# Layer 1 of a two-layer graph network: seven instead of four row tiles a group with head 0's product as an exponential of logs, 19 instead of 22 tiles summed by transfer

## The chip, the cores and the metric

The kernel runs on one core of a Trainium2 chip. The metric is the device time of one execution in microseconds (us). The core's engines each have their own instruction queue: PE (TensorE) multiplies matrices, DVE (VectorE) and ACT (ScalarE) work on tiles element by element, POOL (GpSimd) does too and issues transfers, SP (SyncE) issues transfers. PEld is PE's loading of weights. Everything is in float32.

## The reference, cut to what matters

The change is in layer 1, a graph attention with 8 heads over 4096 nodes. `data` is the layer's normalised input, `connectivity` is `adj` itself, added to the logits.

```python
N, IN_DIM, H, D = (4096, 512, 8, 64)
data1 = (data @ W.T + b).reshape(N, H, D)
src = jnp.einsum('nhd,xhd->nh', data1, src_proj)
trg = jnp.einsum('nhd,xhd->nh', data1, trg_proj)
e = src.T[:, :, None] + trg.T[:, None, :]
e = jnp.where(e >= 0, e, 0.01 * e)
e = e + connectivity[None, :, :]
scores = jax.nn.softmax(e, axis=-1)
out = jnp.einsum('hnm,hmd->hnd', scores, data1.transpose(1, 0, 2))
```

So the numerator of the softmax for head h, target n and source m is exp(leaky(src[n,h] + trg[m,h])) * exp(adj[n,m]). The kernel needs, for each head, its product with `data1` and its sum over m.

## The kernel before, in words

Layer 0 and the linear part of layer 1 take the first 1,660 us and aren't touched. Then comes the attention of layer 1, which the change is in. The work is cut into 8 groups: 4 blocks `b` of WL = 1024 targets, times 2 halves `g` of 4 heads (HG). A group walks over NT = 32 row tiles `m` of 128 sources each. One pair (group `i`, tile `m`) is a step, and the steps of all groups form one long list.

The order of the work is written out by hand: each engine executes its instructions in the order in which the program names them. `stages` says which function runs in a step and how many steps ahead of that step's tile: `load` 4 steps ahead, `exps` 1, `weigh` 1, `factors` 2, `logs` at the step itself, `scale` 2, `gather` 0. In a step s of a group this gives:

- `load` (SP): the tile of `adj_t` four steps ahead into e (4 buffers); in some steps also the next group's z rows (steps 3 and 4, counted by the tile that is loaded) and the next group's u row, broadcast over the partitions (when the tile loaded is 28).
- `exps` (ACT, L1061): ex = exp(adj) of tile s+1, into PSUM, one buffer.
- `weigh` (DVE) of tile s+1: the products pr3, pr0, pr1, pr2 of the four heads, in this order. Heads 1 to 3 are max(z, g_m) times ex (L1107), where head 3 uses e3, an exp with a bias. Head 0 is (rl - ngd_m) * ex (L1104). pr0 has three buffers, pr1 to pr3 have two.
- Also in `weigh`, on POOL: acc3 += pr3 (L1116), and head 0's running sum by transfer: for the tiles in `BY_DMA`, a transfer with an adding write puts pr0 onto one of two accumulators acc00 and acc01 in turn (L1120 for the first two tiles, L1122 for the rest).
- `factors` (ACT) of tile s+2: e3 (L1071), then rl, a relu of z with scale and bias (L1089).
- For the tiles that are keys of `BY_LOG`, head 0 goes another way. `logs` writes lg, a relu of u (the logarithm's part that depends on both, L1078), on ACT in the step that `BY_LOG` names, and a transfer on POOL's queue adds the tile of `adj_t` to it in place (L1079). Two steps ahead of the tile, `relus` takes exp(lg + t_m) straight into pr0 (ACT, L1086) instead of writing rl, and DVE has three products for this tile, not four. lg has one buffer.
- `scale`: in groups 0 and 1 alone, the values of two heads are multiplied by d_m (ACT, L1057, or POOL for the first tiles).
- `gather` (PE) of tile s: 16 matmuls of 32 output columns each for the values (L1139, each is two instructions of the trace), and sums with 2 columns (L1144, `dn`): those of heads 1 and 2 for all tiles, that of head 0 for the tiles that are not in `BY_DMA` (weights `zo`). `side`, the parity of how many such tiles came before, says which half of the output partitions goes first. At the last tile PE also sums the accumulators.

At a group's end ACT copies the four banks of values (os, L1172) and, a step later, dn (od, L1178). The output of a group is finished during the next group: in the steps that `PARTS` names PE transposes (`pt`, L1198; pd, L1182, from od), DVE takes a reciprocal (rd, L1186), ACT scales four pieces (o, L1225) and transfers add x and write out. PE's transposes come behind the gathers of steps 1, 2, 6, 11 and 18, and the four o are written in steps 3, 4, 7, 8, 12, 13, 19 and 20. Group 0 has no such predecessor and makes tables instead, mostly in its first ten steps.

Of the kernel before, what the change touches and what calls it, by code (L numbers as in the profile page):

```python
# [8 lines left out]
FP = mybir.dt.float32  # L9
AF = mybir.ActivationFunctionType  # L10
ALU = mybir.AluOpType
# [4 lines left out]
P = 128  # L16
# [6 lines left out]
def row_bcast(ap, n, offset=0):  # L23

    return bass.AP(tensor=ap.tensor, offset=ap.offset + offset, ap=[[0, P], [1, n]])
# [3 lines left out]
def kernel(  # L29
# [15 lines left out]
    nc = tc.nc  # L45
    N, F = x.shape
    H, D = 8, 64
    HG, WL = 4, 1024
    WT = WL // P
    NT = N // P  # L50
# [14 lines left out]
    u_d = dram.tile([2, NT, P], FP, name="u_d")  # L65
# [39 lines left out]
    with tc.tile_pool(name="w0", bufs=1) as wp, tc.tile_pool(name="a0", bufs=2) as ap_, tc.tile_pool(  # L105
        name="a0s", bufs=8
# [355 lines left out]
    with tc.tile_pool(name="mx", bufs=1) as mxp, tc.tile_pool(name="b_a", bufs=6) as adjp, tc.tile_pool(  # L462
        name="b_e", bufs=1
    ) as esp, tc.tile_pool(name="b_m", bufs=4) as mkp, tc.tile_pool(name="b_s", bufs=2) as sp, tc.tile_pool(
        name="b_p", bufs=6, space=PSUM
# [11 lines left out]
        def load(i, j, t):  # L477
            w, lo, sk = parts(i, j, t)
            rows = slice(t * P, (t + 1) * P)
            ar = adjp.tile([P, BL], FP, name="ar")  # L480
            nc.sync.dma_start(ar[:, :w], adj[rows, lo:lo + w])
            ac = adjp.tile([P, BL], FP, name="ac")
            nc.sync.dma_start(ac[:, :w], adj_t[rows, lo:lo + w])
            loaded[i, j, t] = ar, ac
# [36 lines left out]
        for n in range(-6, len(items)):  # L521
            for f, ahead in ((load, 6), (mask, 1), (scores, 0)):
                if 0 <= n + ahead < len(items):
                    f(*items[n + ahead])
            if n >= 0:
                i, j, t = items[n]
                if j == NB - 1 and t % TB == TB - 1 and i < NB - 1:
                    ends[n + 2] = ends[min(n + 5, len(items) - 2)] = ends[min(n + 7, len(items) - 1)] = \
                        maxima(i, accs[i], p_x, sp)
                    if i < KEEP:  # L530
                        extra.append(support_sums((7, 6, 4)[i // 2], i % 2))
                next(ends.get(n, iter(())), None)
                if extra and next(extra[0], 0) == 0:
                    extra.pop(0)
                if (i, j) == (1, 3) and t % TB == TB - 1:
                    nc.sync.dma_start(mb_0, row_bcast(mx_d[0], BL))
# [7 lines left out]
    with tc.tile_pool(name="c_a", bufs=7) as adjp, tc.tile_pool(name="c_e", bufs=9) as etp, tc.tile_pool(  # L544
        name="c_d", bufs=5
    ) as wkp, tc.tile_pool(name="c_t", bufs=2) as atp, tc.tile_pool(name="c_u", bufs=2) as smp, tc.tile_pool(
        name="c_m", bufs=2
    ) as mxp, tc.tile_pool(name="c_o", bufs=4) as iop, tc.tile_pool(name="c_v", bufs=1) as cvp, tc.tile_pool(
        name="c_s", bufs=2
# [61 lines left out]
        def weigh(b, m):  # L611
            d, i = ex.pop((b, m)), m - b * TB
            if m % 2 == 0:
                at[b, m // 2] = atp.tile([P, 2, BL], FP, name="at")
            w = at[b, m // 2]
            nc.vector.tensor_tensor(w[:, m % 2, :], d, aj.pop((b, m)), ALU.mult)  # L616
            if m == 0:
                racc = blk[b][1] = mxp.tile([P, BL], FP, name="racc")
                nc.gpsimd.memset(racc, 0.0)
            racc, c0 = blk[b][1], max(i + 1, 0) * P  # L620
            if c0 < BL:
                nc.gpsimd.tensor_tensor(racc[:, c0:], racc[:, c0:], d[:, c0:], ALU.add)  # L622
# [247 lines left out]
        def gather(b, m):  # L870
# [5 lines left out]
            elif b:  # L876
                products(b - 1, NT // 2 - 1, PR[NF:])

        stages = ((load, 11), (load_a, 7), (gather, 0), (turn, 5), (exps, 4), (more_sums, 1), (weigh, 2), (sums, 2),
                  (residuals, 0))  # L880
        z = bank(PR[-1])
        pc = column_maxima(acc_z, z)
        dens = iter(())
        for s in range(-11, end):
            b, m = divmod(s, NT)
# [88 lines left out]


    PARTS = (0, 1, 2, 3, 4, 6, 7, 8, 11, 12, 13, 18, 19, 20, 22)
    BY_LOG = {10: 5, 16: 10, 22: 16, 27: 22}
    BY_DMA = [m for m in range(NT) if m not in (4, 7, 13, 14, 19, 23, 24, 25, 29, 31)]

    with tc.tile_pool(name="p", bufs=2) as prp, tc.tile_pool(name="rl", bufs=2) as rlp, tc.tile_pool(  # L980
        name="io1", bufs=2
    ) as iop, tc.tile_pool(name="s1", bufs=1) as sp, tc.tile_pool(name="za", bufs=1) as zp0, tc.tile_pool(name="e3", bufs=2) as e3p, tc.tile_pool(
        name="zb", bufs=1
    ) as zp1, tc.tile_pool(name="e", bufs=4) as ep, tc.tile_pool(name="ac", bufs=2) as acp, tc.tile_pool(
        name="os", bufs=1
    ) as osp, tc.tile_pool(name="u", bufs=1) as usp, tc.tile_pool(
        name="p_x", bufs=1, space=PSUM
    ) as p_x, tc.tile_pool(name="p_v", bufs=1, space=PSUM) as p_v, tc.tile_pool(
        name="p_t1", bufs=1, space=PSUM
    ) as p_t, tc.manual_schedule():  # L990
        groups = [(b, g) for b in range(N // WL) for g in range(H // HG)]
        steps = [(i, m) for i in range(len(groups)) for m in range(NT)]
        us = {}
        zs_, ra, ex, e3, rl, pr, acc, pv, late = {}, {}, {}, {}, {}, {}, {}, {}, {}
# [35 lines left out]
        def zload(i, k):  # L1030
            b, g = groups[i]
            zs_[i, k] = (zp1 if i % 2 else zp0).tile([P, WL], FP, name=f"z{k}")
            nc.sync.dma_start(zs_[i, k], row_bcast(z_d, WL, (g * HG + k) * N + b * WL))

        def load(i, m):
            b, g = groups[i]
            e = ep.tile([P, WL], FP, name="e")
            nc.sync.dma_start(e, adj_t[m * P:(m + 1) * P, b * WL:(b + 1) * WL])
            ra[i, m] = e
            if i + 1 < len(groups) and m == 28:  # L1040
                us[i + 1] = usp.tile([P, WL], FP, name="u")
                b, g = groups[i + 1]
                nc.sync.dma_start(us[i + 1], row_bcast(u_d, WL, g * N + b * WL))
            m0, n = (3, 2) if i else (22, 1)
            if i + 1 < len(groups) and m0 <= m < m0 + HG // n:
                for k in ORDER[n * (m - m0):n * (m - m0) + n]:
                    zload(i + 1, k)
# [26 lines left out]
        def logs(i, s):  # L1074
            for m in [m for m in BY_LOG if BY_LOG[m] == s]:
                b, g = groups[i]
                r = rlp.tile([P, WL], FP, name="lg", bufs=1)
                nc.scalar.activation(r, us[i], AF.Relu, bias=nlg_m[:, g, m:m + 1], scale=-(1.0 - SLOPE))  # L1078
                nc.gpsimd.dma_start(r, adj_t[m * P:(m + 1) * P, b * WL:(b + 1) * WL], accum_op=ALU.add)  # L1079
                rl[i, m] = r  # L1080

        def relus(i, m):
            h = groups[i][1] * HG
            if m in BY_LOG:
                pr[i, m, 0] = prp.tile([P, WL], FP, name="pr0", bufs=3)
# [6 lines left out]
        def weigh(i, m, order=ORDER):  # L1092
            h = groups[i][1] * HG
            x_ = ex.pop((i, m))
            for k in order:
                if (i, m, k) in pr:
                    continue
                w = prp.tile([P, WL], FP, name=f"pr{k}", bufs=3 if k == 0 else 2)
                if k == 0 and (i, m) == (0, 0):
                    r = rlp.tile([P, WL], FP, name="rl")  # L1100
                    nc.vector.tensor_scalar(r, zs_[0, 0], g_m[:, 0, 0:1], d_m[:, 0, 0:1], ALU.max, ALU.mult)
                    nc.vector.tensor_tensor(w, r, x_, ALU.mult)
                elif k == 0:
                    nc.vector.scalar_tensor_tensor(w, rl.pop((i, m)), ngd_m[:, h // HG, m:m + 1], x_,  # L1104
                                                   op0=ALU.subtract, op1=ALU.mult)
                else:
                    nc.vector.scalar_tensor_tensor(w, zs_[i, k], g_m[:, h + k, m:m + 1],  # L1107
                                                   e3.pop((i, m)) if k == 3 else x_,
                                                   op0=ALU.max, op1=ALU.mult)
                pr[i, m, k] = w  # L1110
            w = pr[i, m, 3]
            if m == 1:
                acc[i, 3] = acp.tile([P, WL], FP, name="acc3", bufs=1)
                nc.gpsimd.tensor_tensor(acc[i, 3], pr[i, 0, 3], w, ALU.add)
            elif m > 1:
                nc.gpsimd.tensor_tensor(acc[i, 3], acc[i, 3], w, ALU.add)  # L1116
            if m == 1:
                for n in range(2):
                    acc[i, 0, n] = acp.tile([P, WL], FP, name=f"acc0{n}", bufs=1)
                    nc.gpsimd.dma_start(acc[i, 0, n], pr[i, n, 0])  # L1120
            elif m > 1 and m in BY_DMA:
                nc.gpsimd.dma_start(acc[i, 0, BY_DMA.index(m) % 2], pr[i, m, 0], accum_op=ALU.add)  # L1122

        def gather(i, m):
            b, g = groups[i]
# [4 lines left out]
            v, dn = pv[i]  # L1130
            by_pe = [u for u in range(NT) if u not in BY_DMA]
            side = sum(u < m for u in by_pe) % 2
# [143 lines left out]


        load(0, 0)
        for k in ORDER:
            zs_[0, k] = zp0.tile([P, WL], FP, name=f"z{k}")  # L1280
# [28 lines left out]
        for g in range(H // HG):  # L1309
            nc.gpsimd.tensor_copy(d0_m[:, 2 * g:2 * g + 2, :, 0], d_m[:, HG * g + 1:HG * g + 3, :])  # L1310
        nc.gpsimd.tensor_copy(d0_0[:, :, 0], d0_m[:, :, 0, 0])
        weigh(0, 0, (3, 1, 2, 0))
        scale(0, 0)
        factors(0, 1)
        scale(0, 1)

        stages = ((load, 4), (exps, 1), (weigh, 1), (factors, 2), (logs, 0), (scale, 2), (gather, 0))
        for s in range(len(steps)):
            for f, ahead in stages:
# [48 lines left out]
```

## Time and profile before

| what | value |
|---|---|
| time before, median of 3 runs | 2880.13 us (2878.46 to 2880.64) |
| the profiled execution's own time | 2878.71 us |
| its span, first to last instruction | 2876.9 us |
| PE, DVE, ACT, POOL busy over the span | 2770.8, 2610.5, 1391.4, 1533.9 us |
| layer 1's attention, from first `pv` matmul | from 1672 us to the end |
| L1107 and L1104, DVE, one product of 128 x 1024 | 1.27 us, starts 1.19 us apart |
| L1078 and L1086, ACT, 32 each | 1.135 us |
| L1079, transfer onto lg, 32 | 512 KB each |
| L1120 and L1122, transfer of pr0 onto acc, 16 and 160 | 512 KB each, 5.8 us to landing |

The profile shows one execution. Busy times of an engine are the union of its instructions; an instruction's time includes the part in which the next one already runs, so starts can be closer than durations. A wait is idle time of an engine just before an instruction, with the instruction or transfer that ended it. A transfer's time to landing runs from its issue to the arrival of its last part.

### The profile page before, as it was taken

What the parts mean: (1) busy time and instruction counts of PE and PEld (TensorE: products, weight loads), DVE (VectorE), ACT (ScalarE), POOL (GpSimd) and SP (SyncE); (2) the same over time, 40 slices, a digit from 0 to 9 for tenths busy, and PEclk for the clock granted to TensorE, in tenths of its full rate; (3) what the DMA queues carried; (4) which work ended last, traced back from release to release, by engine and by line L of the source; (5) the groups of instructions that cost most, each with busy time, mean ns of one, the idle gap of its engine ahead of it and who ended that gap; (6) DMA issues with size and microseconds to landing.
All of it is one profiled execution on the core that took longest, in us unless ns stands there. A gap on an engine that the chain in (4) does not pass through costs nothing.

```text
span 2876.9 us, 47763 instructions
## 1 busy us (share of the span) xinstructions
PE 2770.8 (96%) x16859; PEld 1486.0 (52%) x16859; DVE 2610.5 (91%) x3694; ACT 1391.4 (48%) x2116; POOL 1533.9 (53%) x1320
## 2 busy tenths in 40 slices
PE   7999999997999999999998979999999999999998
PEld 4885444444888878878875424322222222222222
DVE  7877798898898898899995799999999999999998
ACT  2212233332223322322321078887878777878786
POOL 5323444443244345345454766676757675757675
PEclk9999999998999999999999989999999999999999
DMA  5538798887999876766754179898989898989896
GB/s 179 175 89 289 249 343 300 292 299 205 199 192 215 224 171 193 210 179 191 207 151 132 51 203 246 237 241 234 235 236 243 234 242 237 241 240 239 212 230 170
DMA packets 528321, 622.60 MB, mean 216 GB/s; under 512 B 294136, under 2 KB 346392, under 8 KB 528080
## 3 DMA queue, kind: packets, MB, share of 16 engines
q1 hardware_dynamic: 461488, 413.00, 48.4%
q0 software_dynamic: 64576, 202.61, 29.8%
q10 hardware_dynamic: 2016, 3.93, 0.4%
q8 instruction: 132, 2.16, 0.3%
q14 instruction: 109, 0.89, 0.1%
HBM read 421.01 MB, written 106.10 MB: 183 GB/s over the span
## 4 chain that ended last, share of the span: by engine, by line
PE 70%; DVE 16%; DMA 6%; issue 5%; ACT 2%; SPq 1%; DVEq 0%; POOL 0%; ACTq 0%; POOLq 0%
PE pv L1139 26%; PE pe L501 14%; PE po L669 11%; PE dn L1144 8%; PE bank L269 6%; PE po L809 4%; DVE pr L1107 4%; DVE at L616 3%; DMA et<-er_d 2%; DVE d L608 2%; DVE u L637 1%; DMA a<-in_adj_t_dram 1%; SPq L581 1%; ACT e L1071 1%; DMA et<-ec_d 1%
## 5 line engine op out<-in xcount | busy, mean ns | idle before, releaser
L1139 PE MATMUL pv<-pr,sup 128*32 128x512 f32 x8192 | 1020.7, 594 | 14.0 <-DMA e<-in_adj_t_dram 10.9
L1116 POOL TENSOR_TENSOR acc<-acc,pr 128x1024 f32<-128x1024 f32 x240 | 572.8, 2387 | 311.5 <-DVE pr L1107 309.8
L1107 DVE SCALAR_TENSOR_TENSOR pr<-z,g_m,ex 128x1024 f32<-128x1024 f32 x512 | 630.1, 1270 | 0.0
L1139 PEld LDWEIGHTS pv<-pr,sup 128*32 128x32 f32 x8192 | 294.0, 110 | 608.7 <-issue 564.7
L609 ACT ACTIVATE d<-d 128x512 f32<-128x512 f32 x256 | 161.1, 630 | 542.1 <-DVE d L608 321.4
L501 PE MATMUL pe<-he_t,he_t 128*128 128x512 f32 x896 | 386.4, 592 | 0.0
L1061 ACT ACTIVATE ex<-e 128x1024 f32<-128x1024 f32 x256 | 263.3, 1028 | 241.7 <-DVE pr L1107 239.2
L1144 PE MATMUL dn<-pr,d_m 128*2 128x512 f32 x1984 | 344.7, 592 | 0.0
L1107 DVE SCALAR_TENSOR_TENSOR pr<-z,g_m,e 128x1024 f32<-128x1024 f32 x256 | 327.3, 1279 | 0.0
L1071 ACT ACTIVATE e<-e,ld_m 128x1024 f32<-128x1024 f32 x256 | 290.7, 1135 | 0.0
L1104 DVE SCALAR_TENSOR_TENSOR pr<-rl,ngd_m,ex 128x1024 f32<-128x1024 f32 x223 | 283.2, 1270 | 1.9 <-ACT ex L1061 1.6
L501 PEld LDWEIGHTS pe<-he_t,he_t 128*128 128x128 f32 x896 | 169.2, 190 | 208.4 <-issue 192.6
L1089 ACT ACTIVATE rl<-z,ngd_m,d_m 128x1024 f32<-128x1024 f32 x223 | 273.8, 1228 | 0.0
L616 DVE TENSOR_TENSOR at<-d,a 128x512 f32<-128x512 f32 x256 | 215.4, 842 | 54.7 <-PE po L669 44.7
L669 PE MATMUL po<-he_t,at 128*128 128x256 f32 x1024 | 263.9, 380 | 0.0
L669 PE MATMUL po<-sup,u 128*128 128x256 f32 x1024 | 262.8, 379 | 0.0
L669 PE MATMUL po<-sup,at 128*128 128x256 f32 x1024 | 244.3, 381 | 13.4 <-DVE at L616 13.4
L622 POOL TENSOR_TENSOR racc<-racc,d 128x512 f32<-128x512 f32 (+2 forms) x136 | 181.0, 1331 | 96.5 <-ACT d L609 91.3
L669 PEld LDWEIGHTS po<-sup,at 128*128 128x128 f32 x1024 | 195.3, 191 | 41.3 <-DVE at L616 14.7
L669 PEld LDWEIGHTS po<-sup,u 128*128 128x128 f32 x1024 | 194.7, 190 | 26.6
L669 PEld LDWEIGHTS po<-he_t,at 128*128 128x128 f32 x1024 | 193.5, 190 | 28.1 <-DVE sc L689 2.3
L506 POOL DMA_DIRECT2D er_d<-mk x136 | 74.4, 547 | 234.8 <-DVE rm L503 227.0
(261 smaller groups left out, 3748.7 us busy)
## 6 DMA issues: line engine op xcount, KB each, us to landing
e<-in_adj_t_dram SPq DMA_DIRECT2D x256, 512.0 KB, 5.9
acc<-pr POOLq DMA_DIRECT2D x176, 512.0 KB, 5.8
a<-in_adj_t_dram SPq DMA_DIRECT2D x256, 256.0 KB, 3.6
ar<-in_adj_dram SPq DMA_DIRECT2D x120, 256.0 KB, 4.8
ac<-in_adj_t_dram SPq DMA_DIRECT2D x120, 256.0 KB, 5.1
ec_d<-mc POOLq DMA_DIRECT2D x120, 256.0 KB, 4.8
et<-ec_d SPq DMA_DIRECT2D x120, 256.0 KB, 3.5
er_d<-mk POOLq DMA_DIRECT2D x112, 256.0 KB, 4.2
```

The lines of the kernel that those rows point to most:

```text
L501: nc.tensor.matmul(pe[:, :w], he_t[i][:, k, (t % TB) * P:(t % TB + 1) * P], he_t[j][:, k, BL - w:], start=(k == 0), stop=(k == KC - 1))
L616: nc.vector.tensor_tensor(w[:, m % 2, :], d, aj.pop((b, m)), ALU.mult)
L622: nc.gpsimd.tensor_tensor(racc[:, c0:], racc[:, c0:], d[:, c0:], ALU.add)
L669: nc.tensor.matmul(acc[:, j, :], A[:, j * P:(j + 1) * P], B, start=(first_ and j == 0), stop=last, skip_group_check=True)
L1061: nc.scalar.activation(x_, ra.pop((i, m)), AF.Exp)
L1071: nc.scalar.activation(x_, ra[i, m], AF.Exp, bias=ld_m[:, h // HG, m:m + 1])
L1089: nc.scalar.activation(r, zs_[i, 0], AF.Relu, bias=ngd_m[:, h // HG, m:m + 1], scale=d_m[:, h, m:m + 1])
L1104: nc.vector.scalar_tensor_tensor(w, rl.pop((i, m)), ngd_m[:, h // HG, m:m + 1], x_, op0=ALU.subtract, op1=ALU.mult)
L1107: nc.vector.scalar_tensor_tensor(w, zs_[i, k], g_m[:, h + k, m:m + 1], e3.pop((i, m)) if k == 3 else x_, op0=ALU.max, op1=ALU.mult)
L1116: nc.gpsimd.tensor_tensor(acc[i, 3], acc[i, 3], w, ALU.add)
L1139: nc.tensor.matmul(v[c][q][r * D + c0:r * D + c0 + Q, :], va[:, m, g * HG + k, c0:c0 + Q], pr[i, m, k][:, q * BL:(q + 1) * BL], start=(m = ...
L1144: nc.tensor.matmul(dn[r * Q:r * Q + w.shape[1], :], w, src[:, q * BL:(q + 1) * BL], **fl)
```

## The change

The table `BY_LOG` gets seven tiles (6, 10, 14, 19, 22, 26, 30), with the steps in which their lg is written (1, 5, 9, 14, 17, 21, 25), in place of four. `BY_DMA` leaves out thirteen tiles instead of ten, so that 19 of 32 are summed by transfer. A group's u row is loaded along with its own first tile, which is four steps later than before, since the last lg of the group before is now written in step 25. The index of the accumulator counts so that the last tile summed by transfer goes onto acc01, as before.

```diff
     PARTS = (0, 1, 2, 3, 4, 6, 7, 8, 11, 12, 13, 18, 19, 20, 22)
-    BY_LOG = {10: 5, 16: 10, 22: 16, 27: 22}
-    BY_DMA = [m for m in range(NT) if m not in (4, 7, 13, 14, 19, 23, 24, 25, 29, 31)]
+    BY_LOG = {6: 1, 10: 5, 14: 9, 19: 14, 22: 17, 26: 21, 30: 25}
+    BY_DMA = [m for m in range(NT) if m not in (2, 4, 8, 12, 13, 16, 17, 18, 21, 24, 25, 28, 31)]
...
             ra[i, m] = e
-            if i + 1 < len(groups) and m == 28:
-                us[i + 1] = usp.tile([P, WL], FP, name="u")
-                b, g = groups[i + 1]
-                nc.sync.dma_start(us[i + 1], row_bcast(u_d, WL, g * N + b * WL))
+            if i and m == 0:
+                us[i] = usp.tile([P, WL], FP, name="u")
+                nc.sync.dma_start(us[i], row_bcast(u_d, WL, g * N + b * WL))
...
             elif m > 1 and m in BY_DMA:
-                nc.gpsimd.dma_start(acc[i, 0, BY_DMA.index(m) % 2], pr[i, m, 0], accum_op=ALU.add)
+                nc.gpsimd.dma_start(acc[i, 0, (len(BY_DMA) + BY_DMA.index(m)) % 2], pr[i, m, 0], accum_op=ALU.add)
```

## The prediction

> **What bounds the kernel now.** The change touches layer 1 alone, so I read first the busy times by stage, in stretches one group long. A group is 32 steps of one row tile each, and groups 2 to 6 repeat every 148.5 us (columns: stretch, length, then busy us and instructions of PE, PEld, DVE, ACT, POOL, the granted clock, the share of the DMA engines, GB/s).
>
> ```profile
> 1675.00:1841.00 166.00, 162.24 (x1464) 57.14 (x1464) 165.17 (x140) 135.28 (x183) 116.70 (x81) 0.98 0.88 233
> 1841.00:1989.70 148.70, 148.63 (x1362) 44.10 (x1363) 148.51 (x126) 128.49 (x192) 99.50 (x61) 1.00 0.92 239
> 2138.30:2286.80 148.50, 148.43 (x1360) 44.06 (x1363) 148.32 (x126) 115.91 (x138) 99.69 (x61) 1.00 0.93 239
> ```
>
> PE and DVE are both full, so the question is what each can do alone. Next I read the timeline of DVE (start, us, instruction).
>
> ```profile
> 2166.01 1.27 DVE L1107 SCALAR_TENSOR_TENSOR pr<-z,g_m,e 128x1024 f32<-128x1024 f32 x1
> 2167.20 2.46 DVE L1107 SCALAR_TENSOR_TENSOR pr<-z,g_m,ex 128x1024 f32<-128x1024 f32 x2
> 2169.59 1.30 DVE L1107 SCALAR_TENSOR_TENSOR pr<-z,g_m,e 128x1024 f32<-128x1024 f32 x1
> 2170.82 1.27 DVE L1104 SCALAR_TENSOR_TENSOR pr<-rl,ngd_m,ex 128x1024 f32<-128x1024 f32 x1
> 2172.01 2.46 DVE L1107 SCALAR_TENSOR_TENSOR pr<-z,g_m,ex 128x1024 f32<-128x1024 f32 x2
> ```
>
> Its instructions start 1.19 us apart without a hole: 4 in an ordinary step (4.77 us), 3 in the step of a log tile (2166.01 to 2169.59, 3.58 us). 124 of them are 147.9 us; the reciprocal and one wait of 0.18 us for ex make up the rest. Then the timeline of PE, where L1144 `zo` is head 0's sum of a tile that no transfer adds up.
>
> ```profile
> 2145.94 1.04 PE L1144 MATMUL dn<-pr,d_m 128*2 128x512 f32 x8
> 2146.80 0.60 PE L1144 MATMUL dn<-pr,zo 128*2 128x512 f32 x2
> 2146.81 0.60 PE L1139 MATMUL pv<-pr,sup 128*32 128x512 f32 x2
> 2147.23 0.60 PE L1144 MATMUL dn<-pr,zo 128*2 128x512 f32 x2
> ...
> 2154.53 0.60 PE L1144 MATMUL dn<-pr,d_m 128*2 128x512 f32 x2
> 2154.95 0.60 PE L1139 MATMUL pv<-pr,sup 128*32 128x512 f32 x2
> 2154.96 1.45 PE L1144 MATMUL dn<-pr,d_m 128*2 128x512 f32 x6
> 2156.34 0.66 PE L1198 MATMUL pt<-ident,os 128*128 128x128 f32 x4
> ```
>
> PE starts four narrow matmuls together every 0.429 us; I call that a round. A step is 32 + 8 matmuls, 10 rounds, 4.29 us. `zo` adds four matmuls, half of two rounds (2146.80, 2147.23), filled up by the next `pv`: one round in all. Where a stretch between two transposes `pt` holds an odd number of such additions, its last four run two by two: the x6 at 2154.96 takes three rounds' room for one and a half, 0.43 us lost. Per group that is 333 rounds' worth, three such losses (before `pt` of steps 6 and 11, and at the next group's first `dn`), and the transposes. The rounds keep their 0.429 us throughout; the spacings that are longer without a transpose's own reason add up to 0.2 us (0.595 against 0.531 before the first `dn`, which waits for od, and 0.681 against 0.543 before the `pt` that waits for rd). So PE has 148.3 us of work of its own in 148.5. Last, ACT's timeline; the bracket is its idle time.
>
> ```profile
> 2214.66 0.90 ACT L1225 ACTIVATE o<-pt,rd 128x64 f32<-128x64 f32 x4
> 2216.30 1.03 ACT L1061 ACTIVATE ex<-e 128x1024 f32<-128x1024 f32 x1 [0.73 <-DVE pr L1107]
> 2224.65 1.03 ACT L1061 ACTIVATE ex<-e 128x1024 f32<-128x1024 f32 x1 [0.35 <-DVE pr L1107]
> 2227.79 1.13 ACT L1078 ACTIVATE lg<-u,nlg_m 128x1024 f32<-128x1024 f32 x1
> 2229.47 1.03 ACT L1061 ACTIVATE ex<-e 128x1024 f32<-128x1024 f32 x1 [0.55 <-DVE pr L1107]
> ```
>
> ACT has 1.54 us of idle in an ordinary step, 0.73 where it also writes four o, 0.55 where it writes an lg, and only 0.35 in DVE's short step. ex has one buffer, so what ACT does beyond that idle holds up DVE's next product.
>
> The Trainium skill (Perfetto Trace Analysis, Identifying the Most-Contended Engine) judges TensorE by the share of its weight loads, not by its matmul time, and the other engines by occupancy. By that rule PE at 44.06 of 148.5 us has room, DVE is the engine to relieve, and the sum would be the full DVE saving, 28.6 us. The spacing of the rounds speaks against it, and I go by the rows.
>
> **The change part by part**, per group, against 148.53 us.
>
> *DVE.* Three head-0 products fall out: 3 x 1.19 = -3.58 us.
>
> *PE.* 13 tiles instead of 10 are summed by PE: +3 rounds, 1.29 us. The stretches now hold (by m) 2 | 4 | 8 | 12, 13, 16, 17, 18 | 21, 24, 25, 28, 31 and the three of the accumulators: odd four times where it was three: +0.43. If the 0.2 us of waits go, PE's own time is 148.33 + 1.72 = **150.05, +1.5 us**. Bounds: +0.9 (no fourth loss, no waits left) and +1.9 (waits also grow).
>
> *ACT.* Three tiles more cost one ACT instruction each, 1.13 us (the lg; the exponential takes the place of rl). 116 of 148.5 us leave room in the mean, but the place decides: lg is written in steps 1, 5, 9, 14, 17, 21, 25, and DVE's short steps are now 5, 9, 13, 18, 21, 25, 29. In four of them (5, 9, 21, 25) the lg, 1.0 us net of overlap, meets 0.35 us of idle: 0.6 us each. In step 13 four o (0.8 net) meet it: 0.45. Before, no lg and no o fell into a short step (9, 15, 21, 26). Sum 2.85, and 0.05 us for each short step as now: 3.0.
>
> *Transfers.* 26 transfers of 512 KB go out on POOL's queue per group before and after: three acc fewer, three lg more, POOL's 0.86 us for each and its busy time unchanged. What changes is a wait. pr0 has three buffers, and ACT writes a log tile's pr0 two steps ahead, into the buffer of tile m-3. Before, m-3 (7, 13, 19, 24) was never a tile that a transfer reads; now it is one in six cases of seven (3, 7, 11, 19, 23, 27), each sent one step after an lg. The nearest rows are the acc transfers of tile 18, also sent one step after an lg.
>
> ```profile
> DMA to landing us min/median/max: 8.7/8.7/8.7
> DMA to landing us min/median/max: 9.5/9.5/9.5
> DMA to landing us min/median/max: 9.4/9.4/9.4
> DMA to landing us min/median/max: 8.2/9.9/11.4
> ```
>
> Those are tile 18's in groups 3, 4 and 7; the last row is all lg of groups 1 to 6. From the issue at 2205.64 to ACT's third instruction two steps later, at 2213.53, are 7.9 us: ACT would wait 0.8 to 1.6 us, more after a short step. Queued behind the waiting exponential are o and the next ex, for which DVE waits. Covered by ACT's idle in steps 24 and 28 (1.54), half in steps 8 and 12 (0.73). I take 1.0 us each for m = 10 and 14, 0.4 for the rest: 2.4. Bounds: 0, where all land as fast as the acc median of 5.9; 14, where all take its longest 11.0 us (6 x 2.4). The lg must land too: 13.2 us lie between its relu and its exponential now (2227.79 to 2241.01), some 12.6 then, against 1.4 + 9.9.
>
> So the DVE and ACT side is 148.53 - 3.58 + 3.0 + 2.4 = **150.35, +1.8 us**, beside PE's +1.5.
>
> *At no cost.* The u load moves from step 24 to step 28 of the group before, on SP behind one e load: SP only issues there, u (9.4 us to landing) is first needed in step 1, five steps or 23 us on; without that cover lg in step 1 would hold ACT. The other index for acc only alternates two accumulators as before.
>
> *Groups 0 and 1.* There ACT also scales `sup`, 0.57 us in each step, so the collisions cost 4 x 1.17 + 1.0 and the transfer waits 1.1 more: +5.8 us (some 4.9 in group 0, which has no o). PE takes up a product 1 to 2.6 us after it is written (the last of tile 10 ends at 2169.66, its matmuls start at 2171.97), which swallows up to 2 us: I take +3.5 each.
>
> *Sum.* 6 x 1.9 + 2 x 3.5 = **+18 us** on the profiled execution's 2878.7 (span 2876.9 and 1.8 around it); the median of the runs lies 1.4 above it, so **2898 us**. The case's own range is 2888 (only PE's +1.5, less in group 0) to 2912 (ACT's waits twice as long).
>
> **The rivals.** *DVE's saving comes through: faster.* The waits by engine show PEld waiting for pr 11 times, 3.2 us, in one group. If those were true stalls of PE, its own work would be 145.3, then 147.0; with ACT's collisions hidden in the products written ahead, a group takes 147.0: 8 x -1.5, **2868 us**. It decides once PE's work is under 146.8 us. Against it: the matmul rounds do not move at those places. 8%.
>
> *No change: the gains and losses meet.* The added `zo` fills slots that idle now and the waits are hidden: **2880 us**, 0.5 either way per group. Against it: three lost half rounds are all the idle slots there are. 9%.
>
> *The transfers set the pace.* If each of the six exponentials waits for a late acc by 1.2 us beyond its cover, the DVE side is 148.0 + 7: +5.8 a group, **2925 us**. For it: the DMA engines are at 0.93 already. Against it: the transfers are no more than before. 10%.
>
> My case has 73%. The range is 2881 to 2918: it takes in about half of no change and of the slow rival. A measurement of this kernel can tell about 0.2%, 5.8 us: faster 0.08, same 0.09, slower 0.83.
>
> **What would show it.** DVE x123 instead of x126 in a group's stretch, but the group 150 to 151 us long, PE still full, rounds at 0.429 us; the x6 `dn` before `pt` four times; DVE idle for ex or pr, 0.6 us in steps 5, 9, 21, 25; ACT idle ahead of L1086 for acc. Groups under 148 us, or PE with holes while DVE is full, would make it wrong.

## The result, and the profile after

| | time, us | runs |
|---|---|---|
| before | 2880.39 (2878.46 to 2880.69) | 4 |
| after | **2928.7** (2923.27 to 2933.26) | 4 |

The ratio is 1.0168 [1.0149, 1.0188]: 48.3 us slower. The forecast of 2898 us had the sign, and neither the size nor the range (2881 to 2918).

First the profile's page after the change: span, busy times, and the head of the chain of waits that ended last, by engine.

```profile
span 2924.7 us, 47804 instructions
PE 2802.8 (96%) x16955; PEld 1510.2 (52%) x16955; DVE 2593.5 (89%) x3670; ACT 1412.2 (48%) x2140; POOL 1536.1 (53%) x1320
PE 45%; DVE 23%; DMA 12%; issue 7%; ACT 7%; POOL 3%; SPq 2%; DVEq 0%; ACTq 0%; POOLq 0%
acc<-pr POOLq DMA_DIRECT2D x152, 512.0 KB, 6.7
```

DVE has 24 instructions fewer and is busy for 17 us less than before (2610.5), and the span is 47.8 us longer. PE is still "96% busy", as before. The chain tells more: before, 70% of it was PE and 6% DMA; now PE is down to 45%, DVE, ACT and DMA together are 42%. The median time to landing of the transfers onto acc went from 5.8 to 6.7 us although there are 24 fewer of them.

Next the windows by stage, three groups in a row from first `pv` to first `pv` (the columns are those of the prediction: stretch, length, busy us and instructions of PE, PEld, DVE, ACT, POOL, granted clock, DMA share, GB/s).

```profile
1829.50:1986.10 156.60, 152.90 (x1375) 47.41 (x1371) 146.36 (x123) 131.95 (x199) 101.81 (x63) 1.00 0.87 226
1986.10:2140.30 154.20, 152.06 (x1373) 44.20 (x1368) 146.21 (x123) 118.35 (x141) 99.95 (x61) 1.00 0.89 228
2140.30:2295.90 155.60, 152.69 (x1376) 45.72 (x1373) 146.36 (x123) 118.34 (x142) 100.12 (x61) 1.00 0.89 228
```

DVE has its x123, as foretold, but the group takes 154 to 157 us, not 150. DVE is idle for 8 to 10 us of it, PE for 2 to 4, and the DMA engines are *less* busy than before (0.89 instead of 0.93): each of them waits for something. The clock is 1.00. Over the eight groups, from first `pv` to first `pv` (group 7 up to its last `pv`):

| group | 0 | 1 | 2 | 3 | 4 | 5 | 6 | 7 |
|---|---|---|---|---|---|---|---|---|
| before, us | 152.31 | 149.02 | 148.52 | 148.53 | 148.52 | 148.53 | 148.83 | 147.23 |
| after, us | 154.11 | 156.63 | 154.21 | 155.56 | 154.77 | 154.41 | 156.59 | 150.09 |

The differences sum to 44.9 us. Another 2.9 lie ahead of the first group, where nothing was changed; that part differs from run to run.

What they wait for is in the waits by engine from 1670 us on (engine, instruction, what ended the wait: us in total, times, longest):

```profile
ACT pr L1085 <- DMA acc<-pr: 77.2, 33, 4.8
PEld pv L1138 <- DVE pr L1106: 59.6, 93, 2.1
DVE pr L1106 <- ACT ex L1060: 43.6, 28, 3.1
DVE pr L1103 <- ACT ex L1060: 16.3, 34, 1.5
```

Line numbers after the change are one lower: L1085 is the exponential that writes a log tile's pr0, L1060 is ex, L1103 and L1106 are DVE's products. Before, the first of these rows did not exist. Now ACT stands 77.2 us before its log exponential, in 33 of 56 cases, each time until a transfer onto acc has landed; by its timeline the wait is 85.9 us in 38 cases, since the profile books five such waits on PE or on nothing, although they too end within 0.2 us of a landing. The next two rows are the same time handed on: DVE waits for the ex that stands behind the exponential in ACT's order, and PE for DVE's products. The last row is something else: head 0's product waits for ex behind a short step of DVE in which ACT also wrote an lg or four o. These are the collisions of the prediction, and experiment 6 shows them alone.

One such wait in full, from the timeline of group 3 around tile 14 (start, us, engine, instruction; in brackets the idle time before it and what ended it):

```profile
2188.49 1.38 POOL L1121 DMA_DIRECT2D acc<-pr  x1
2189.55 1.21 POOL L1078 DMA_DIRECT2D lg<-in_adj_t_dram  x1
...
2192.61 1.39 POOL L1121 DMA_DIRECT2D acc<-pr  x1
...
2199.64 1.13 ACT L1070 ACTIVATE e<-e,ld_m 128x1024 f32<-128x1024 f32 x1
...
2203.33 1.28 DVE L1106 SCALAR_TENSOR_TENSOR pr<-z,g_m,e 128x1024 f32<-128x1024 f32 x1
...
2204.87 1.15 ACT L1085 ACTIVATE pr<-lg,t_m 128x1024 f32<-128x1024 f32 x1 [4.10 <-DMA acc<-pr]
2205.93 0.91 ACT L1224 ACTIVATE o<-pt,rd 128x64 f32<-128x64 f32 x4
2206.72 1.04 ACT L1060 ACTIVATE ex<-e 128x1024 f32<-128x1024 f32 x1
...
2207.79 2.47 DVE L1106 SCALAR_TENSOR_TENSOR pr<-z,g_m,ex 128x1024 f32<-128x1024 f32 x2 [3.18 <-PE dn L1143]
```

The first three lines are three transfers in a row on POOL's queue: tile 10's pr0, tile 14's lg, tile 11's pr0. (A fourth, which adds x to an o of 256 KB, was sent ahead of them at 2185.41.) Their landings, one by one in the same order:

```profile
DMA to landing us min/median/max: 6.0/6.0/6.0
DMA to landing us min/median/max: 10.3/10.3/10.3
DMA to landing us min/median/max: 12.2/12.2/12.2
```

They land at 2194.5, 2199.9 and 2204.8. The exponential of tile 14 writes into the buffer of tile 11's pr0 and starts at 2204.87, as soon as the third has landed. Behind it come o and ex; ex ends at 2207.76 and DVE's next product starts at 2207.79, after 3.18 us without work. The profile puts that last wait down to PE's `dn`, but what ended just before it is ex.

### The profile page after: what moved, and what is told of

It is laid out like the page before. It is cut to its first block, busy times and chain, and to the rows that moved or that the text cites. A ratio compares the mean times of both kernels' runs of the same rounds, so it can differ in the third digit from the quotient of the medians.

```text
span 2924.7 us, 47804 instructions
## 1 busy us (share of the span) xinstructions
PE 2802.8 (96%) x16955; PEld 1510.2 (52%) x16955; DVE 2593.5 (89%) x3670; ACT 1412.2 (48%) x2140; POOL 1536.1 (53%) x1320
## 4 chain that ended last, share of the span: by engine, by line
PE 45%; DVE 23%; DMA 12%; issue 7%; ACT 7%; POOL 3%; SPq 2%; DVEq 0%; ACTq 0%; POOLq 0%
PE pe L501 13%; PE po L669 11%; DVE pr L1106 10%; PE pv L1138 8%; DMA acc<-pr 6%; PE bank L269 6%; PE po L809 4%; DVE at L616 3%; PE dn L1143 3%; POOL acc L1115 3%; DMA et<-er_d 2%; ACT e L1070 2%; DVE pr L1103 2%; DVE d L608 2%; ACT rl L1088 1%
## 5 line engine op out<-in xcount | busy, mean ns | idle before, releaser
L1115 POOL TENSOR_TENSOR acc<-acc,pr 128x1024 f32<-128x1024 f32 x240 | 595.7, 2482 | 290.9 <-DVE pr L1106 290.9
L1106 DVE SCALAR_TENSOR_TENSOR pr<-z,g_m,ex 128x1024 f32<-128x1024 f32 x512 | 631.1, 1273 | 46.9 <-ACT ex L1060 43.6
L1138 PEld LDWEIGHTS pv<-pr,sup 128*32 128x32 f32 x8192 | 303.0, 110 | 623.0 <-issue 492.5
L1060 ACT ACTIVATE ex<-e 128x1024 f32<-128x1024 f32 x256 | 263.1, 1028 | 180.3 <-DVE pr L1106 177.8
L1143 PE MATMUL dn<-pr,d_m 128*2 128x512 f32 x1984 | 338.2, 592 | 0.0
L1106 DVE SCALAR_TENSOR_TENSOR pr<-z,g_m,e 128x1024 f32<-128x1024 f32 x256 | 333.7, 1303 | 0.0
L1103 DVE SCALAR_TENSOR_TENSOR pr<-rl,ngd_m,ex 128x1024 f32<-128x1024 f32 x199 | 253.5, 1274 | 17.2 <-ACT ex L1060 16.3
L1088 ACT ACTIVATE rl<-z,ngd_m,d_m 128x1024 f32<-128x1024 f32 x199 | 245.2, 1232 | 0.0
```

The source lines that it names most:

```text
L1060: nc.scalar.activation(x_, ra.pop((i, m)), AF.Exp)
L1088: nc.scalar.activation(r, zs_[i, 0], AF.Relu, bias=ngd_m[:, h // HG, m:m + 1], scale=d_m[:, h, m:m + 1])
L1138: nc.tensor.matmul(v[c][q][r * D + c0:r * D + c0 + Q, :], va[:, m, g * HG + k, c0:c0 + Q], pr[i, m, k][:, q * BL:(q + 1) * BL], start=(m = ...
L1143: nc.tensor.matmul(dn[r * Q:r * Q + w.shape[1], :], w, src[:, q * BL:(q + 1) * BL], **fl)
```

## The experiments

Each kernel was timed beside the kernel before on the same chip: 2880.01 us for the first four, 2879.56 for the others.

**1. A fourth buffer for pr0.** With four, the exponential writes into the buffer of tile m-4, one step older. Space for it came from rl, which has one buffer here instead of two.

```diff
-                pr[i, m, 0] = prp.tile([P, WL], FP, name="pr0", bufs=3)
+                pr[i, m, 0] = prp.tile([P, WL], FP, name="pr0", bufs=4)
...
-            r = rlp.tile([P, WL], FP, name="rl")
+            r = rlp.tile([P, WL], FP, name="rl", bufs=1)
...
-                w = prp.tile([P, WL], FP, name=f"pr{k}", bufs=3 if k == 0 else 2)
+                w = prp.tile([P, WL], FP, name=f"pr{k}", bufs=4 if k == 0 else 2)
...
```

> The changed kernel with four buffers for pr0 (the room comes from rl, one buffer instead of two), all else as in the changed kernel. The exponential of log tile m then waits for the transfer of pr0 of tile m-4, sent a step earlier, not for that of m-3. If the waits of ACT for those transfers (77.2 us, 33 times in the changed kernel's layer 1) set the time, they go and the kernel takes 2890 to 2900 us, what is left being PE's +1.5 us a group and ACT's collisions. If the collisions of lg with DVE's short steps or PE's added sums set it, it stays at 2920 to 2930 us.

Measured: 2897.92 us (2895.99 to 2899.12), ratio 1.0061 [1.0045, 1.0077]. The row "ACT pr L1085 <- DMA acc" is gone from the waits. In its place are small ones:

```profile
ACT rl L1088 <- DVE pr L1103: 44.8, 142, 1.2
DVE pr L1103 <- ACT ex L1060: 22.1, 27, 1.7
```

The first is the price of the single rl buffer, 0.3 us a time. Neither row costs time in a group such as this, where PE has no idle:

```profile
2129.70:2280.40 150.70, 150.70 (x1372) 45.76 (x1369) 145.68 (x122) 120.92 (x141) 99.70 (x62) 1.00 0.91 235
```

The transfers themselves are no faster. All those onto acc take 6.9 us to landing in the median (6.7 in after), and those of the tiles three before log tiles 10, 14, 22, 26 and 30 still take 8.1 to 11.7 us in groups 1 to 6. So what cost the time is that ACT waited for them. Without that wait 31 of the 48 us are gone, and groups 3 to 6 take 150.7 us. Of the 17.9 us that are left, experiment 3, which has PE's part alone, shows 15.7.

**2. The same number of sums, other tiles.** PE again sums 13 tiles, among them m-3 of every log tile, so that no exponential follows a transfer.

```diff
-    BY_DMA = [m for m in range(NT) if m not in (2, 4, 8, 12, 13, 16, 17, 18, 21, 24, 25, 28, 31)]
+    BY_DMA = [m for m in range(NT) if m not in (3, 4, 7, 11, 13, 16, 17, 19, 21, 23, 25, 27, 31)]
```

> The changed kernel with the thirteen tiles that PE sums chosen so that all of 3, 7, 11, 16, 19, 23, 27, the tiles three before a log tile, are among them: no exponential waits for a transfer any more, and PE has as many sums as in the changed kernel (two odd stretches instead of four, 0.9 us a group less). If the wait sets the time: 2882 to 2894 us. If the seven lg, their transfers or ACT's collisions do: 2915 us or more.

Measured: 2885.09 us (2883.96 to 2886.99), ratio 1.0019 [1.0009, 1.0028]. One group in the windows:

```profile
2284.00:2433.00 149.00, 149.00 (x1372) 45.09 (x1368) 145.29 (x123) 118.89 (x141) 99.98 (x61) 1.00 0.92 237
```

With as many logs and as many sums, 43.6 of the 48.7 us between after and the kernel before are gone through the choice of tiles alone. This choice also has two odd stretches instead of four, so it takes away both the wait and some of PE's lost rounds at once; experiment 3 says how much is which. PE is now full (149.00 of 149.00) and DVE is not.

**3. The change to PE alone.** After's sums with the four log tiles of before; DVE has its 126 instructions.

```diff
-    BY_LOG = {6: 1, 10: 5, 14: 9, 19: 14, 22: 17, 26: 21, 30: 25}
+    BY_LOG = {10: 5, 16: 10, 22: 16, 27: 22}
```

> The second half of the change alone: the four log tiles of before, 19 tiles summed by transfer. DVE has its 148.5 us a group as before and PE 150.0. If PE's sums cost what its rounds say: +1.5 us a group, 2888 to 2896 us. If they fill idle slots: 2878 to 2884 us. If they are most of the 48 us: over 2915 us. One log tile of four (27, by the transfer of 24: not sent; 10 by 7, 16 by 13 of which 13 is not sent, 22 by 19) can wait for a transfer: those of 7 and 19.

Measured: 2895.67 us (2895.03 to 2896.45), ratio 1.0054 [1.0038, 1.007]. In the windows:

```profile
2128.50:2279.20 150.70, 150.70 (x1373) 45.31 (x1372) 149.39 (x126) 115.98 (x138) 97.08 (x58) 1.00 0.87 225
```

PE alone takes +2.2 us a group, where +1.5 was forecast. PE's timeline shows why, in the group's last step and ahead of the first `pt` of the next group (step 1):

```profile
2277.50 0.60 PE L1143 MATMUL dn<-pr,d_m 128*2 128x512 f32 x2
2277.89 0.60 PE L1138 MATMUL pv<-pr,sup 128*32 128x512 f32 x2
2277.93 1.42 PE L1143 MATMUL dn<-pr,d_m 128*2 128x512 f32 x6
2279.18 0.60 PE L1143 MATMUL dn<-acc,zo 128*2 128x512 f32 x2
2279.19 0.62 PE L1138 MATMUL pv<-pr,sup 128*32 128x512 f32 x2
...
2287.57 1.23 PE L1143 MATMUL dn<-pr,d_m 128*2 128x512 f32 x6
2288.72 0.95 PE L1181 MATMUL pt<-pick,od 128*128 128x8 f32 x7
```

The two `pv` at 2277.89 and the six `dn` behind them are eight matmuls, two rounds' worth, and take until 2279.18, 1.29 us or three rounds: the first `dn` run beside the `pv`, the last four two by two. That is one lost round of 0.43 us, in a stretch that the prediction counted as even. With 13 sums ahead of it, `side` is the other way round at tile 31, so the last tile's sum and the accumulators' meet on the same half of the output partitions. The same stretch loses another round at its end, ahead of the `pt` at 2288.72. By the starts of its matmuls PE loses a round in six places of a group here (the last step, and ahead of the `pt` of steps 1, 2, 6, 11 and 18), where the kernel before has three and the prediction four. Three more sums (1.29 us) and three more lost rounds (1.29), less the 0.2 us of waits that the prediction expected to go and that are gone, make 2.4; 2.2 were measured.

Experiment 2 has as many sums and loses a round in two places. PE is full in both, at 149.07 and 150.73 us a group: 1.66 us for four places, or some 13 us in all. With the 31 of experiment 1 that makes 44, what experiment 2 gave back.

Of the two log tiles whose m-3 goes by transfer here (10 and 22), tile 10 waits for its acc in every group, 10.7 us in the profile's row, but at 150.7 PE is full all the same.

**4. The logs alone.** After's seven log tiles with the sums of before.

```diff
-    BY_DMA = [m for m in range(NT) if m not in (2, 4, 8, 12, 13, 16, 17, 18, 21, 24, 25, 28, 31)]
+    BY_DMA = [m for m in range(NT) if m not in (4, 7, 13, 14, 19, 23, 24, 25, 29, 31)]
```

> The first half alone: seven log tiles, 22 tiles summed by transfer, so PE's work is that of before (148.3 us a group) and 29 transfers go out on POOL's queue instead of 26. Four of the seven log tiles follow three behind a tile that is sent (3, 11, 16, 27). If the waits for transfers set the time: about four sixths of the changed kernel's 9.7 us a group, 153 us a group, 2900 to 2920 us. If PE's added sums did: 2876 to 2884 us. If the number of transfers did: more than the changed kernel, over 2930 us.

Measured: 2918.11 us (2914.65 to 2919.59), ratio 1.0128 [1.011, 1.0146]; a group takes 151 to 157 us. The waits have

```profile
ACT pr L1085 <- DMA acc<-pr: 35.5, 17, 4.1
ACT pr L1085 <- PE pv L1138: 15.0, 7, 3.4
```

The new log tiles alone cost 38 us, with no further sum on PE. The +38 here and the +16 of experiment 3 add up to 54, near the change's 48. That is no clean sum: here only four log tiles (6, 14, 19 and 30) follow a transfer, not six. That PE's longer work is partly hidden where the transfers hold up ACT fits the two, but isn't shown by them.

**5. The wait alone, on the kernel before.** Four logs and ten sums by PE as before; only, tiles 7, 13, 19 and 24 (m-3 of the log tiles) now go by transfer, and four others by PE.

```diff
-    BY_DMA = [m for m in range(NT) if m not in (4, 7, 13, 14, 19, 23, 24, 25, 29, 31)]
+    BY_DMA = [m for m in range(NT) if m not in (4, 8, 12, 14, 20, 22, 23, 25, 29, 31)]
```

> The kernel before with one thing changed: four other tiles are summed by PE, so that the tiles three before the log tiles (7, 13, 19, 24) go by transfer; as many sums, transfers, logs and odd stretches as before. If an exponential's wait for the transfer of the tile three before it is what costs, it appears here too: in full where that transfer follows an lg by one step (log tiles 10 and 27, 1 to 3 us each), less for 16 and 22, whose lg has a step more; 1 to 5 us a group, 2886 to 2915 us. If the change's loss needs its seven lg or its sums on PE: 2878 to 2883 us.

Measured: 2896.81 us (2893.43 to 2900.01), ratio 1.0059 [1.0045, 1.0073].

```profile
ACT pr L1086 <- DMA acc<-pr: 15.2, 9, 3.3
ACT pr L1086 <- PE dn L1144: 11.4, 10, 2.3
```

17 us from nothing but which tiles are summed how; three stretches are odd, as before. In groups 1 to 7 ACT waits 1.5 to 2.4 us where the acc takes 9.3 to 10.2 to landing (tile 10), 0.8 to 2.2 us at 8.7 to 10.1 (tile 27), 0.6 to 1.2 us at 8.5 to 9.0 (tile 22), and not at all at 5.2 to 6.1 (tile 16). All these waits together are 32.5 us; the profile puts 11.4 of them to PE's `dn` in the second row and 6.0 to nothing, though each ends within half a microsecond of its transfer's landing.

**6. The collisions alone, on the kernel before.** The lg of three of its log tiles is written one step earlier, so that they fall into DVE's short steps 9, 15 and 21.

```diff
-    BY_LOG = {10: 5, 16: 10, 22: 16, 27: 22}
+    BY_LOG = {10: 5, 16: 9, 22: 15, 27: 21}
```

> The kernel before with three of its four lg written one step earlier, in steps 9, 15 and 21, where DVE has only three products; nothing else is changed. If ACT's collision costs what the changed kernel shows (0.56 us each, DVE's starts 1.75 instead of 1.19 us apart), DVE's side is 148.5 + 1.7 us a group: 2890 to 2895 us. If the products written ahead swallow it: 2879 to 2882 us.

Measured: 2894.13 us (2893.6 to 2895.36), ratio 1.0051 [1.0037, 1.0064]. A group takes 150.1 us, +1.6; DVE's product that meets a collision starts 1.75 us after the last one instead of 1.19. The waits show what the prediction named, DVE waiting for ex, where the kernel before has 1.6 us in 8 cases:

```profile
DVE pr L1104 <- ACT ex L1061: 14.4, 31, 0.9
```

**7. lg a step earlier in after.** For tiles 10, 14, 26 and 30 the lg goes out one step before DVE's short step.

```diff
-    BY_LOG = {6: 1, 10: 5, 14: 9, 19: 14, 22: 17, 26: 21, 30: 25}
+    BY_LOG = {6: 1, 10: 4, 14: 8, 19: 14, 22: 17, 26: 20, 30: 24}
```

> The changed kernel with four of its lg (of tiles 10, 14, 26, 30) one step earlier, in steps 4, 8, 20, 24: out of DVE's short steps, and their transfers two steps ahead of that which the exponential waits for. If the wait is long because that transfer stands right behind the lg in POOL's queue: the waits fall from 77 us to under 30, 2896 to 2908 us. If the exponential waits that long for any transfer of the tile three before: 2915 us or more.

Measured: 2910.96 us (2908.17 to 2911.84), ratio 1.0105 [1.009, 1.0121], a little above what was expected.

```profile
ACT pr L1085 <- DMA acc<-pr: 35.0, 18, 3.6
```

More than half of the wait in this row is gone, 77.2 to 35.0 us (85.9 to 43.4 by the timeline), with the same transfers. Tiles 26 and 30 are cured (their acc land in some 7 us). In groups 1 to 7 tiles 10 and 14 still wait 1.0 to 3.1 us, with landings of 8.8 to 10.9: just ahead of their lg, by 1 and 3.1 us in group 3, another acc goes out, and ahead of those of 26 and 30 none for 7 us. Tile 22's lg wasn't moved, and its wait stayed.

The 18 us that the run gains are not all the wait's, since it takes the collisions away too:

```profile
DVE pr L1106 <- ACT ex L1060: 41.2, 28, 3.8
DVE pr L1103 <- ACT ex L1060: 4.1, 15, 0.7
```

Against after, the first row, what ACT's wait hands on, fell by 2.4 us only (43.6, with 3.2 more that were booked on PE); the second, the collisions, by 12.2 (16.3). By these rows most of the gain is the collisions'. By the timeline DVE's idle behind the exponentials of tiles 14 and 26 fell from 31.0 to 3.8 us, while behind those of 10 and 22 it grew from 15.5 to 36.1; why it grew is not shown.

**8. Five logs, placed by what the others showed.** No lg in a short step, no transfer into a log tile's buffer, 27 transfers, ten sums by PE.

```diff
-    BY_LOG = {6: 1, 10: 5, 14: 9, 19: 14, 22: 17, 26: 21, 30: 25}
-    BY_DMA = [m for m in range(NT) if m not in (2, 4, 8, 12, 13, 16, 17, 18, 21, 24, 25, 28, 31)]
+    BY_LOG = {7: 1, 12: 5, 17: 10, 23: 17, 29: 23}
+    BY_DMA = [m for m in range(NT) if m not in (4, 5, 8, 9, 13, 14, 20, 24, 26, 31)]
```

> A version by the same accounts: five log tiles (7, 12, 17, 23, 29), each three behind a tile that PE sums, lg never in a short step of DVE or in one with four o, ten tiles summed by PE with one odd stretch instead of three. DVE's side is 123 products, 147.4 us a group, PE's 147.5: 2870 to 2876 us, below the kernel before. If more logs cost by themselves (27 transfers for 26): over 2882 us.

Measured: **2871.8 us** (2870.11 to 2873.88, 7 runs), ratio 0.9972 [0.9961, 0.9983]. It beats both kernels.

```profile
1973.30:2120.70 147.40, 147.40 (x1360) 46.96 (x1356) 147.21 (x124) 116.41 (x138) 100.84 (x62) 1.00 0.94 241
2268.70:2416.10 147.40, 147.40 (x1360) 44.79 (x1356) 147.22 (x125) 117.08 (x139) 100.68 (x62) 1.00 0.94 242
```

A group takes 147.4 us (group 3 148.0) with PE and DVE both full, one product less than before; no L1085 waits for an acc. PE loses a round in one place instead of three, which with the waits that went is 0.86 + 0.2 us a group, and DVE's product less is 1.19: either side alone would have held the group near its old 148.5, and it took both.

## Why the prediction was wrong, point by point

**The failed step is the size of the transfer wait**, "I take 1.0 us each for m = 10 and 14, 0.4 for the rest: 2.4", and with it the range "(ACT's waits twice as long)". The mechanism was right: pr0's third buffer, six of seven tiles, o and ex behind the exponential. Groups 1 to 6 take 155.4 us in the mean; without the wait the same sum gives 148.53 - 3.58 + 3.0 = 148.0. By this sum the wait is worth 7.4 us a group and not 2.4, within the bounds of 0 to 14 that were stated for it but outside the range made from them. DVE's own idle agrees: in groups 2 to 6 it stands 7.1 us a group before the products that need the ex behind an exponential. Experiment 1, which takes this wait away, gives 2897.9 us; it gets back 4.4 us a group and no more because PE then bounds the group at 150.7.

Why it was too small: "ACT would wait 0.8 to 1.6 us" was read from three landings of tile 18's acc, 8.7, 9.5 and 9.4 us, and three of the four shortest were taken. In groups 0, 2, 5 and 6 of the same trace it took longer:

```profile
DMA to landing us min/median/max: 12.0/12.0/12.0
DMA to landing us min/median/max: 10.3/10.3/10.3
DMA to landing us min/median/max: 11.0/11.0/11.0
DMA to landing us min/median/max: 10.7/10.7/10.7
```

With group 1's 9.4 the mean of the eight is 10.1; less the 7.9 us after which ACT is ready, that is a wait of 2.2 us in the mean, and up to 4.1. The waits of after are 1.6 to 2.6 us at tile 10 from group 1 on, 2.0 to 4.1 at 14, 1.3 to 2.5 at 22, 1.7 to 4.8 at 26, up to 2.0 at 30, none at 6 (nor at 19, whose buffer PE releases): in the mean 85.9 / 38 = 2.3 us. So the row chosen was the right one, and much of the error lies in which of its values were read. The rest is in what was taken off for ACT's idle: the four tiles 6, 22, 26 and 30 were to cost 0.4 us a group together, and in groups 2 to 6 DVE idles 2.4 us behind tile 26 and 0.8 behind tile 22.

The order in the queue does the rest at single tiles. For tiles 10, 14, 26 and 30 DVE's short step lies between the lg and the acc, which follows the lg by 2.9 to 3.1 us instead of the 3.9 of tile 18, and the longest landings are at two of them, 10.5 to 12.2 us at tile 14 and 9.7 to 12.9 at 26 (from group 1 on). But the short step isn't what makes tile 10 wait: in experiments 3 and 5 its acc follows the lg by 3.85 us and it waits 1.5 to 2.5 us as well. Experiment 7 shows that the place of the lg matters: with the same transfers half of ACT's wait is left. That each acc is late just because the lg before it isn't done yet is the reading of the landings; no run moved the lg off POOL's queue.

**"The transfers set the pace", 2925 us, was what came.** It had 10%. Its price, 1.2 us beyond ACT's cover for each of six tiles, is what was measured: 7.4 / 6. (Its own sum is off: 148.0 + 7 is +6.5 a group and not +5.8, which would have been some 2932.) The argument against it, "the transfers are no more than before", was true and beside the point: acc transfers landed as late before, 8.7 to 12.0 us at tile 18, but no exponential waited for them, and in experiment 1 they land as late again at no cost. What was new was the wait, not the lateness.

**PE's +1.5** was 0.7 too little (+2.2 in experiment 3, also above the bound of +1.9). The odd stretches were counted rightly up to the group's last, which was taken as even and lost a round at both ends: six lost rounds instead of four. (One is 0.43 us as the prediction has it, but its "x6" is not one and a half rounds' work: with the two `pv` beside it, eight matmuls, two rounds' worth, take three.) It didn't show in after, where the DVE and ACT side is longer, but it is what bounds experiment 1: PE at 150.7 us. That this run gives the forecast's 2898 is thus partly chance: the prediction got there by 150.35 on the other side.

**DVE's -3.58** came (x123), and **the collisions** were sized rightly: "0.6 us each" against 1.75 - 1.19 = 0.56, and +1.6 a group against 1.7 in experiment 6. In after they came to less than the 3.0 that was summed: in groups 2 to 6 DVE idles 0.4 to 0.5 us at two of the four, less than 0.1 at the other two, which come right behind a wait for an exponential, and 1.3 us at all of them with the four o. So the split of after's loss between collisions and wait is not exact.

**Groups 0 and 1**: +3.5 each was taken; +1.8 and +7.6 came. In group 0 ACT waits only 4.0 us, so less went wrong there than thought. Group 1 has 9.6 us of wait and the scaling of `sup` on top, and loses as much as the later groups. Group 7 lost 2.9 with 9.8 us of wait; DVE idles only 5.1 us in it, against 8.7 in groups 2 to 6, and why stays open.

**The u load and the other accumulator index** cost nothing that any row shows: no lg waits for u.

**DVE's saving comes through, 2868 us**, fell with experiment 3: with DVE's work as before, PE's added rounds move the time by 15.7 us at once. This also answers the rule of the Trainium skill (Perfetto Trace Analysis, Identifying the Most-Contended Engine): by weight loads, 45.31 of 150.7 us here, TensorE has room; the measured time says that it hasn't. (The page names MFU, the arithmetic done against the peak, beside the weight loads; no view here gives it.)

## What to carry to other kernels

When an engine starts to write into a buffer that a transfer used to have to itself, work out which tile's transfer releases it, and price it by the landing of that very transfer in its place in the queue, with what is sent just ahead of it; a median over all transfers, or a few rows picked from the nearest one, is too kind: take all its landings. Where many assignments compute the same thing, the choice of tiles can be worth more than the work saved: experiments 2 and 8 keep the idea of the change and give back 44 and 57 us. On a kernel with two full engines, a saving on one is worth at most the room that the other has.

## What the runs showed of the hardware

Transfers of 512 KB with an adding write, three of them sent on one queue within 4.2 us, land one after another: 6.0, 10.3 and 12.2 us after their issue, at 2194.5, 2199.9 and 2204.8, some 5 us apart. Sent after the ones before it had landed, the same kind of transfer takes 4.6 us (tile 5's acc in group 3 of after). That the third in a row takes nearly twice the median of 6.7 while the DMA engines as a whole are at 0.89 had not been expected.

Narrow matmuls that find no work on the other half of the output partitions run two by two: in experiment 3, two `pv` and six `dn` took 1.29 us, three rounds instead of two. With the same count of sums, experiments 2 and 3 differ by four such places a group, and PE's time by 1.66 us.
